# Layer one of a two-layer conditioned encoder: softmax sums from ScalarE's accumulator, spread as logarithms, in place of sums by matmul and a division

## The chip, the cores and the metric

The kernel runs on one core of one Trainium2 chip. The metric is the device time of one execution in microseconds (us). Engines are called as the profile calls them: PE (TensorE, matmuls), PEld (its weight loads), DVE (VectorE), ACT (ScalarE), POOL (GpSimd), SP (the queue of most transfers).

## The reference

Two layers on x of 32 batches x 128 tokens x 512 features, with a condition vector of 512 per batch. Cut to what matters (B = 32, N = 128, D = 512, 16 heads of 32):

```python
# layer one
h   = gamma(cond) * layernorm(x) + beta(cond)
q, k, v = split(h @ Wqkv.T + bqkv)             # 16 heads of 32 features
energy  = einsum('bhqd,bhkd->bhqk', q, k)
att     = softmax(energy, axis=-1) / D ** 0.5
h1      = einsum('bhqk,bhkd->bhqd', att, v) @ Wp.T + bp + x
x1      = (gamma(cond) * layernorm(h1) + beta(cond)) + h1
# layer two
h   = film(rmsnorm(x1), cond)                  # one attention head of 512 features
x2  = x1 + softmax(Q K^T * D**-0.5) V @ proj + b
out = x2 + gelu(film(rmsnorm(x2), cond) @ W1 + b1) @ W2 + b2
```

All is float32. Products that need the precision are made of three matmuls in the kernel: each operand is split into a high part (type fp32r) and a low part (the rest), and high x high, high x low and low x high are summed (`mm3`).

## The kernel before

The batches form eight groups of G = 4; a tile of a group has 128 partitions and 4 x 128 = 512 columns. Layer one is a loop of STEPS = 32: step s stands for group s // 4 and feature chunk c = s % 4, that is, four heads of 32 features for four batches at once. The order of the instructions on PE, DVE, ACT and POOL is the order in which the Python code writes them (`tc.manual_schedule`); only SP's queue is ordered by the framework. Each engine takes its own in order, and semaphores hold one back until its inputs and its buffers are ready.

For the softmax, a step works as a pipeline over three neighbouring steps:

- `qk0(s + 2)` makes queries and keys, features on partitions (12 matmuls each, copied out by ACT with the bias, L558).
- `energies(s + 1)` multiplies them per head and batch, with queries on partitions: 16 small matmuls into four PSUM banks `pse` (one for each head r; L575). DVE takes the negated maximum over the keys of each (L587) into `nm`, 128 x 16, and splits it into a high and a low part in `nmx` (L588, L589).
- `maxima(s + 1)` transposes `nmx` on PE (`psm`, L594); `spread_maxima(s + 1)` lays it out on DVE so that a matmul can add it to each column (L600).
- `scores0(s)` computes the scores once more with keys on partitions (`pst`, L616), into four banks that a matmul has first filled with the negated maxima (L612). `exponentials(s)` takes exp of each bank on ACT (L626): `e`.
- `heads_out(s - 1)` multiplies values by `e` (`pso`, L639). Four more matmuls multiply a constant `rootd`, 32 columns of sqrt(D), by `e` (`pss`, L644): the sum over the keys times sqrt(D), repeated on each head's 32 partitions. ACT takes the reciprocal as exp(-ln(.)) (L649, L650).
- `divided0(s - 1)`, on DVE, makes one Newton step for the reciprocal and multiplies (L657, L658, L659). ACT makes the high part for the projection (L661), POOL the low part (L662).

Beside this, each step carries one batch of the other work:

- The next input tile (`Turned`): `stats` and `norm` (DVE, with a power on POOL, L338), `halves` (ACT, L423, then a transposing transfer on SP), one step later `merge` (DVE, L432) and `rest` (four ACT activations, L449), then `high` (ACT, L461) and, at the next step's start, `low` (DVE, L465).
- The values of one batch (`values0`: 12 matmuls, copied by ACT, L542).
- From step 4, the projection of a batch of the group before (`End`: 12 matmuls `psp`, `add` on DVE, L693) and, one step later, the second normalization: `first` (statistics, a product on DVE, L707, an add on POOL, L708), `second` (DVE, L712), `third` (DVE, L721).
- From step 4 to 27, layer two's weights (`Weights`: ACT copies L936, POOL differences L943 and sums L929).

PSUM has eight banks in three pools: `mm_tile` (2), `s_tile` (2), `e_bank` (4). The scores take the two of `mm_tile` and the two of `s_tile`; the energies all four of `e_bank`. Between them the banks hold queries, keys, values, the heads, the sums, the maxima and the projection.

The order in the loop before, other work left out:

```python
energies(s + 1); scores0(s); heads_out(s - 1); exponentials(s)
divided0(s - 1)
run(q); maxima(s + 1); spread_maxima(s + 1); run(k)
run(end.stream())
run(values0(s - 1 + G))
```

Layer two's softmax (`softmax1`, L847) takes exp on 128 columns at a time with the negated maximum as bias and the accumulator's sum as second output.

Of the kernel before, what the change touches and what calls it, by code (L numbers as in the profile page):

```python
# [9 lines left out]
FP = mybir.dt.float32  # L10
# [28 lines left out]
RIGHT_LOW_LAST = ((0, 0), (1, 0), (0, 1))  # L39


@with_exitstack
def cond_seq_kernel(ctx: ExitStack, tc, x, condT, wcond, w0, w1, wk1, wm1, wm2, cols, rows, out):
# [68 lines left out]
    rootd = const.tile([P, HD], FP, name="rootd")  # L112
    nc.vector.memset(rootd, float(D) ** 0.5)
# [39 lines left out]
    def mm3(make, terms, done=None, by_part=False):  # L153

        if by_part:
            calls = [(a[pa], b[pb]) for pa, pb in RIGHT_LOW_LAST for a, b in terms]
        else:
            calls = [(a[pa], b[pb]) for a, b in terms for pa, pb in PARTS]
# [233 lines left out]
    class Turned:  # L392
# [66 lines left out]
        def high(self):  # L459
            if self.layer < 2:  # L460
                nc.scalar.copy(self.hi, self.dst)  # L461
# [42 lines left out]
    qk, vs, es, os_, mT = {}, {}, {}, {}, {}  # L504
# [45 lines left out]
    def qk0(s, by_part=False):  # L550
# [5 lines left out]
        for a, (nm, bias) in enumerate((("q", C_BQ0), ("k", C_BK0))):  # L556
            def done(ps, a=a, bias=bias):
# [5 lines left out]
                lambda nm=nm: (e_bank if nm == "q" and s > 1 else mm_tile)(f"ps{nm}{s}"),  # L563
# [5 lines left out]
    def energies(s):  # L569
# [14 lines left out]
        t = nmx  # L584
        nm = sm.tile([P, 4, G], FP, tag="nm", name=f"nm{s}")
        for r in range(4):
            nc.vector.tensor_reduce(nm[:, r], chunks(banks[r]), AX.X, ALU.max, negate=True)  # L587
        nc.vector.tensor_copy(t[:, :, :G].bitcast(FR), nm)  # L588
# [33 lines left out]
    def exponentials(s):  # L622

        for r in range(4):
# [4 lines left out]
    def heads_out(s):  # L629
# [5 lines left out]
        pso, pss = e_bank(f"pso{s}"), e_bank(f"pss{s}")  # L635
# [7 lines left out]
        for r in range(4):  # L643
            nc.tensor.matmul(  # L644
                pss[32 * r : 32 * r + 32], rootd, e[r], start=True, stop=True
            )

        w = p_tile(f"rs{s}")
        nc.scalar.activation(w, pss, AF.Ln)  # L649
        nc.scalar.activation(w, w, AF.Exp, scale=-1.0)  # L650
        es[s] = pso, pss, w

    def divided0(s):

        g, c = divmod(s, KC)
        pso, pss, w = es.pop(s)
        nc.vector.tensor_tensor(pss, pss, w, ALU.mult)  # L657
        nc.vector.tensor_tensor(w, pso, w, ALU.mult)  # L658
        nc.vector.scalar_tensor_tensor(w, pss, 2.0, w, ALU.subtract, ALU.mult, reverse0=True)  # L659
        hi, lo = (t[:, c] for t in os_[g])  # L660
        nc.scalar.copy(hi, w)  # L661
        nc.gpsimd.tensor_tensor(lo, w, hi.bitcast(FP), ALU.subtract)  # L662

    class End:
# [15 lines left out]
        def stream(self):  # L680
            g, i = divmod(self.b, G)

            def done(ps):
# [3 lines left out]
                lambda: mm_tile(f"psp{self.b}"),  # L687
                [(sub(os_[g], k, ts(i, P)), sub(W0["p"], k)) for k in range(KC)],
                done,
# [145 lines left out]
    def softmax1(g):  # L835
# [3 lines left out]
        nm = sm.tile([P, G], FP, tag="nm", name=f"nm1_{g}")  # L839
# [371 lines left out]
    with tc.manual_schedule(engines=ordered):  # L1211
# [65 lines left out]
        for k in range(KC):  # L1277
            product_end(k)
        for p in first:
# [361 lines left out]
```

## Time and profile before

| | |
|---|---|
| median of 3 runs | 1433.27 us (1433.21 to 1435.66) |
| the profiled execution | 1433.07 us, span 1431.3 us |
| busy, whole span | PE 1424.1, PEld 1144.8, DVE 1023.8, ACT 755.8, POOL 437.0 us |
| granted PE clock | 1.000 |
| layer one's loop | about 48 to 532 us of the span |
| sums matmuls, L644 | 256 rows of 592 ns, first at 63.5, last at 532.0 us |
| ACT exponentials, L626 | 128, mean 595 ns |
| DVE maxima, L587 | 128, mean 683 ns |

How to read the profile: an instruction's row has its start, its duration, its engine, its line of the kernel, and what it writes and reads by the program's names. Rows of neighbours on one engine overlap, so the time that an instruction costs its engine is better read from the start of one to the start of the next. Matmuls with 32 rows or 32 columns run side by side, four at a time. In a line of groups, "xN | busy, mean ns" is followed by the engine's idle time just before those instructions and by what ended it. In the chain that ended last each stretch is put down to the engine whose work or whose wait released the next.

### The profile page before, as it was taken

To read this page: it belongs to the slowest core of one execution; us is meant where nothing else is said; L and a number is where in the kernel's file an instruction comes from. 1 tells how busy PE (TensorE), PEld (TensorE's weight loads), DVE (VectorE), ACT (ScalarE), POOL (GpSimd) and SP (SyncE) were. 2 spreads that over 40 slices of the span, in tenths; PEclk is the share of its full clock that TensorE was granted. 3 is DMA by queue.
4 is the path that set the end of the run, shared out by engine and by line. 5 is a ranking of instruction groups with operands and counts; after the bars stand their busy time and mean duration, and the time that the engine had idled before them with its cause. 6 is when DMAs were issued, how large, how long until landed. Compare 5 with 4: busy or idle time off the path is not lost.

```text
span 1431.3 us, 24842 instructions
## 1 busy us (share of the span) xinstructions
PE 1424.1 (99%) x9224; PEld 1144.8 (80%) x9224; DVE 1023.8 (72%) x1909; ACT 755.8 (53%) x1392; POOL 437.0 (31%) x393
## 2 busy tenths in 40 slices
PE   9999999999999999999999999999999999999998
PEld 5777777777777768888888888888888888888887
DVE  6778889878888877999987766755566556743442
ACT  4566665665665546777874544434453444423231
POOL 0124555645645434566551223000030003110000
PEclk9999999999999999999999999999999999999999
DMA  8356788786667576778878867667693777735450
GB/s 313 106 185 160 194 209 221 190 199 176 165 170 189 136 236 184 179 214 232 206 203 338 285 198 255 231 191 220 192 333 122 226 217 223 275 125 179 151 184 30
DMA packets 227874, 287.83 MB, mean 201 GB/s; under 512 B 107396, under 2 KB 138244, under 8 KB 226216
## 3 DMA queue, kind: packets, MB, share of 16 engines
q1 hardware_dynamic: 209888, 211.68, 50.4%
q10 hardware_dynamic: 17864, 74.55, 16.1%
q8 instruction: 73, 1.20, 0.3%
q14 instruction: 49, 0.40, 0.1%
HBM read 193.18 MB, written 73.60 MB: 186 GB/s over the span
## 4 chain that ended last, share of the span: by engine, by line
PE 95%; DVE 3%; ACT 1%; POOL 0%; issue 0%; ACTq 0%; POOLq 0%; DVEq 0%
PE acc L1067 24%; PE psh L165 21%; PE psV L165 6%; PE psT L165 6%; PE psq L165 6%; PE psp L165 6%; PE psk L165 5%; PE psv L165 5%; PE pso L639 2%; PE pse L575 2%; PE pst L616 2%; PE pss L644 2%; PE pss L828 2%; PE pso L165 2%; PE psvp L767 1%; PE psm L744 1%
## 5 line engine op out<-in xcount | busy, mean ns | idle before, releaser
L338 POOL TENSOR_TENSOR rn<-vn,neghalf 128x1 f32<-128x1 f32 x96 | 71.1, 741 | 424.6 <-DVE vn L336 350.1
L423 ACT COPY tn<-x 128x1024 uint16<-128x1024 uint16 x90 | 93.9, 1044 | 68.6 <-DVE x L409 54.4
L1005 ACT ACTIVATE c<-c,col 128x512 f32<-128x512 f32 x64 | 46.4, 725 | 141.9 <-DVE c L1030 88.4
L587 DVE TENSOR_REDUCE nm<-pse 128x4 f32<-128x512 f32 x128 | 79.5, 683 | 45.2 <-PE pse L575 45.2
L1083 POOL TENSOR_TENSOR xe<-xe,row 128x512 f32<-128x512 f32 x32 | 45.3, 1445 | 200.8 <-DMA xe<-xs 144.5
L432 DVE COPY tn<-tn 128x1024 uint16<-128x1024 uint16 x90 | 92.2, 1024 | 0.9 <-DMA tn<-tn 0.9
L1020 DVE TENSOR_TENSOR c<-psh,ca 128x512 f32<-128x512 f32 x32 | 22.1, 691 | 87.0 <-PE psh L165 85.8
L626 ACT ACTIVATE e<-pst 128x512 f32<-128x512 f32 x128 | 65.3, 595 | 1.3 <-PE pst L616 1.3
L409 DVE TENSOR_SCALAR x<-x,rn 128x512 f32<-128x512 f32 x64 | 60.3, 943 | 7.8 <-POOL rn L338 7.2
L943 POOL TENSOR_TENSOR wml<-wm,wmh 128x512 fp32r<-128x512 f32 x28 | 35.5, 1276 | 99.3 <-ACT wmh L936 89.6
L326 DVE BATCH_NORM_STATS2 stn<-x 128x6 f32<-128x512 f32 x96 | 65.4, 682 | 0.1
L649 ACT ACTIVATE rs<-pss 128x512 f32<-128x512 f32 x32 | 19.1, 598 | 80.0 <-PE pss L644 80.0
L338 POOL TENSOR_TENSOR re<-ve,neghalf 128x1 f32<-128x1 f32 x32 | 31.7, 991 | 95.9 <-DVE ve L331 90.3
L449 ACT ACTIVATE tn<-tn,mods 128x128 f32<-128x128 f32 x128 | 52.6, 483 | 11.7 <-DVE tn L432 11.7
L1033 DVE TENSOR_TENSOR ca<-psh,ca 128x512 f32<-128x512 f32 x32 | 22.1, 691 | 42.4 <-PE psh L165 42.4
L449 ACT ACTIVATE tn<-tn,mod 128x128 f32<-128x128 f32 x104 | 42.9, 483 | 15.9 <-DVE tn L432 15.8
L678 POOL TENSOR_TENSOR xe<-xe,row 128x512 f32<-128x512 f32 x32 | 44.5, 1390 | 3.3 <-DMA xe<-in_x 2.8
L1005 ACT ACTIVATE cb<-cb,col 128x512 f32<-128x512 f32 x32 | 23.2, 725 | 41.6 <-DVE cb L1034 41.6
L1087 DVE TENSOR_TENSOR xe<-acc,xe 128x512 f32<-128x512 f32 x32 | 21.1, 688 | 32.4 <-PE acc L1067 32.4
L575 PEld LDWEIGHTS pse<-qk 32*128 32x128 f32 x1024 | 32.0, 186 | 12.2 <-issue 9.6
L1017 ACT COPY ca<-psh 128x512 f32<-128x512 f32 x32 | 18.4, 574 | 42.8 <-PE psh L165 42.2
L1026 DVE TENSOR_TENSOR cb<-psh,ca 128x512 f32<-128x512 f32 x32 | 22.1, 690 | 24.8 <-PE psh L165 24.6
(1387 smaller groups left out, 4703.7 us busy)
## 6 DMA issues: line engine op xcount, KB each, us to landing
mod<-mod SPq DMA_DIRECT2D x32, 512.0 KB, 5.2
ur<-ud SPq DMA_DIRECT2D x64, 256.0 KB, 4.2
xs<-xe SPq DMA_DIRECT2D x60, 256.0 KB, 2.9
xe<-xs SPq DMA_DIRECT2D x60, 256.0 KB, 3.1
x<-xs SPq DMA_DIRECT2D x59, 256.0 KB, 3.7
scw<-scw SPq DMA_DIRECT2D x32, 256.0 KB, 4.1
hTd<-tn SPq DMA_DIRECT2D x32, 256.0 KB, 6.7
hT<-hTd SPq DMA_DIRECT2D x32, 256.0 KB, 4.9
```

The source lines that it names most:

```text
L165: nc.tensor.matmul(st["ps"], *calls[j], start=(j == 0), stop=(j == n - 1))
L326: nc.vector.bn_stats(st, t)
L338: nc.gpsimd.tensor_tensor(r, v, neghalf, ALU.pow)
L409: nc.vector.tensor_scalar(X, X, r, None, ALU.mult)
L423: nc.scalar.copy(halves.rearrange("p (e d) -> p e d", e=2), X.bitcast(U16).rearrange("p (d e) -> p e d", e=2),)
L432: nc.vector.tensor_copy(self.a.bitcast(U16).rearrange("p (f e) -> p e f", e=2), self.t.bitcast(U16).rearrange("p (e f) -> p e f", e=2),)
L449: nc.scalar.activation(dst[:, c], self.a[:, ts(c, P)], AF.Identity, bias=m[:, q + B : q + B + 1], scale=m[:, q : q + 1],)
L575: nc.tensor.matmul(banks[r][:, ts(i, P)], q[32 * r : 32 * r + 32, ts(i, P)], k[32 * r : 32 * r + 32, ts(i, P)], start=True, stop=True,)
L587: nc.vector.tensor_reduce(nm[:, r], chunks(banks[r]), AX.X, ALU.max, negate=True)
L626: nc.scalar.activation(e, es[s][r], AF.Exp)
L1005: nc.scalar.activation(t[nm], t[nm], AF.Gelu, bias=col[:, C_B1 + f : C_B1 + f + 1], scale=1.0)
L1067: nc.tensor.matmul(accs[i], u[pa][:, ts(i, P)], wb[f // 4][pb][:, f % 4, :], start=(first and j == 0), stop=(last and j == len(PARTS) - 1),)
```

## The change

After the change, layer one's sums over the keys come from the energies, which have the queries on partitions. `totals(s, r)` takes exp in place, in the PSUM bank, 128 columns at a time: 16 ACT instructions in a step, each with the negated maximum as bias and with the accumulator's sum as output. `logs(s)` takes the logarithm of sqrt(D) times these sums, corrects it once (exp of its negative on ACT, two small operations on DVE) and subtracts it from the negated maxima. What is transposed and spread is then maximum and logarithm together, so that `exponentials` gives the finished attention. `heads_out` has no sums matmuls, `divided0` is gone; `heads_high` (ACT) and `heads_low` (DVE, before POOL) split the product straight from PSUM. The turned tile's high copy (`turned.high`) goes from ACT to DVE. Banks are dealt out anew: heads and queries in `mm_tile`, keys and values in `s_tile`, maxima and projection in `e_bank`. The order in the loop changes too.

The diff, without the part before the loop and the steps' rarer work:

```diff
-    rootd = const.tile([P, HD], FP, name="rootd")
-    nc.vector.memset(rootd, float(D) ** 0.5)
...
         if by_part:
-            calls = [(a[pa], b[pb]) for pa, pb in RIGHT_LOW_LAST for a, b in terms]
+            order = PARTS if by_part == "left" else RIGHT_LOW_LAST
+            calls = [(a[pa], b[pb]) for pa, pb in order for a, b in terms]
...
-                lambda nm=nm: (e_bank if nm == "q" and s > 1 else mm_tile)(f"ps{nm}{s}"),
+                lambda nm=nm: (s_tile if nm == "k" and s > 1 else mm_tile)(f"ps{nm}{s}"),
...
+    def totals(s, r):
+
+        banks, nm, total = sums0[s]
+        for i in range(G):
+            e = banks[r][:, ts(i, P)]
+            nc.scalar.activation(
+                e, e, AF.Exp, bias=nm[:, r, i : i + 1], scale=1.0,
+                accum_out=total[:, r, i : i + 1],
+            )
+
+    def logs(s):
+
+        _, nm, total = sums0.pop(s)
...
+        nc.scalar.activation(lg, total, AF.Ln, scale=ROOTD)
+        nc.scalar.activation(inv, lg, AF.Exp, scale=-1.0)
+        nc.vector.scalar_tensor_tensor(inv, total, ROOTD, inv, ALU.mult, ALU.mult)
+        nc.vector.scalar_tensor_tensor(lg, inv, -1.0, lg, ALU.add, ALU.add)
+        nc.vector.tensor_tensor(nm, nm, lg, ALU.subtract)
+        t = nmx
         nc.vector.tensor_copy(t[:, :, :G].bitcast(FR), nm)
         nc.vector.tensor_tensor(t[:, :, G : 2 * G], nm, t[:, :, :G], ALU.subtract)
...
-        pso, pss = e_bank(f"pso{s}"), e_bank(f"pss{s}")
+        pso = mm_tile(f"pso{s}")
...
-        for r in range(4):
-            nc.tensor.matmul(
-                pss[32 * r : 32 * r + 32], rootd, e[r], start=True, stop=True
-            )
-
-        w = p_tile(f"rs{s}")
-        nc.scalar.activation(w, pss, AF.Ln)
-        nc.scalar.activation(w, w, AF.Exp, scale=-1.0)
...
-        nc.vector.tensor_tensor(pss, pss, w, ALU.mult)
-        nc.vector.tensor_tensor(w, pso, w, ALU.mult)
-        nc.vector.scalar_tensor_tensor(w, pss, 2.0, w, ALU.subtract, ALU.mult, reverse0=True)
+        nc.scalar.copy(os_[g][0][:, c], es[s])
+
+    def heads_low(s):
...
-        nc.scalar.copy(hi, w)
-        nc.gpsimd.tensor_tensor(lo, w, hi.bitcast(FP), ALU.subtract)
+        nc.vector.tensor_tensor(lo, es.pop(s), hi.bitcast(FP), ALU.subtract)
...
-                lambda: mm_tile(f"psp{self.b}"),
+                lambda: e_bank(f"psp{self.b}"),
                 [(sub(os_[g], k, ts(i, P)), sub(W0["p"], k)) for k in range(KC)],
-                done,
+                done, "left" if i == 0 else False,
```

The loop's order after, as code (the steps' rarer work left out):

```python
scores0(s)
turned.high(nc.vector.tensor_copy); turned.low(nc.vector)
energies(s + 1)
exponentials(s, (0, 1)); totals(s + 1, 0); exponentials(s, (2, 3))
for r in range(1, 4): totals(s + 1, r)
heads_out(s - 1)
past.first(); past.sums(); new.stats(); end.bias(); end.more(); past.second()
ready.merge(); logs(s + 1); heads_high(s - 1)
run(q); run(k)
new.norm(); new.halves()
run(values)                      # steps 0 to 3: 7 of the 12, the rest behind the maxima
maxima(s + 1); spread_maxima(s + 1)
heads_low(s - 1); ready.rest(); past.third()
run(end.stream()); end.add()
weights.heads(wj); weights.tails(wj); weights.sums(wj + 1)
```

Before the loop, the energies, the sixteen exponentials and the logarithms of step 0 are put among the first values, queries and keys in the same way. The four products of layer two's value weights (`vp`, L767) are spread over steps 29 to 31 in another order, with their loads.

## The prediction

> **What bounds the kernel now.** I read the page first: the busy line, then the shares of the chain that ended last.
>
> ```profile
> PE 1424.1 (99%) x9224; PEld 1144.8 (80%) x9224; DVE 1023.8 (72%) x1909; ACT 755.8 (53%) x1392; POOL 437.0 (31%) x393
> ...
> PE 95%; DVE 3%; ACT 1%; POOL 0%; issue 0%; ACTq 0%; POOLq 0%; DVEq 0%
> ```
>
> The chain is PE's own stream almost everywhere, so a matmul that goes is worth its time, if nothing else becomes late. The change lies in layer one's 32 steps, so I asked for busy times over 19 whole steps in its middle (columns: stretch, length, PE, PEld, DVE, ACT, POOL).
>
> ```profile
> 151.62:443.42 291.80, 291.80 (x2984) 230.37 (x2984) 249.29 (x460) 177.73 (x325) 157.44 (x129) 1.00 0.73 192
> ```
>
> Divided by 19, a step is 15.36 us: PE busy for all of it, DVE 13.12, ACT 9.35, POOL 8.29, at full clock. DVE, not ACT, is next. Then the timeline of PE at a step's start:
>
> ```profile
> 243.76 1.17 PE L575 MATMUL pse<-qk 32*128 32x128 f32 x32
> 244.67 0.57 PE L612 MATMUL pst<-mT,over 32*128 32x512 f32 x4
> 244.99 1.15 PE L616 MATMUL pst<-qk 32*128 32x128 f32 x32
> 246.06 1.08 PE L639 MATMUL pso<-e,v 128*32 128x128 f32 x32
> 246.96 1.04 PE L644 MATMUL pss<-e,rootd 128*32 128x512 f32 x8
> 247.93 0.50 PE L165 MATMUL psq<-n_12h,w0qh 128*128 128x512 f32 x1
> ```
>
> From start to start: energies 0.91, scores 1.39, heads 0.90, sums 0.97.
>
> **PE: what goes.** The four sums matmuls (L644) leave each step: 246.96 to 247.93, 0.97. PE's step becomes 14.39. The other matmuls change place and bank, not number. If PE stayed the only bound, 32 x 0.97 = 31 us would go.
>
> **ACT: what comes.** The nearest row for an accumulating exponential on 128 columns is layer two's softmax:
>
> ```profile
> 570.48 0.37 ACT L847 ACTIVATE e<-pss,nm 128x128 f32<-128x128 f32 x1 [3.50 <-DVE nm L843]
> 570.74 0.19 ACT L847 ACTIVATION_READ_ACCUMULATOR e<-pss,nm 128x1 f32 x1
> 570.84 0.36 ACT L847 ACTIVATE e<-pss,nm 128x128 f32<-128x128 f32 x1
> ...
> 571.86 0.70 ACT L793 ACTIVATE T<-psT,cq 128x512 f32<-128x512 f32 x1
> ```
>
> Four pairs take 571.86 - 570.48 = 1.38, 0.345 a pair, though the durations add to 0.57. The 16 new pairs cost 5.52 a step. Theirs write to PSUM, which no ACT row here does; bounds are 0.26 (start to read, 570.74 - 570.48) and 0.57 (no overlap). I take 0.345: same form, and DVE's in-place product in PSUM (L657, 0.693) costs what the one into SBUF does (L658, 0.692).
>
> The logarithm and its exponential are now 128x16. From L649 (512 columns, 0.60) and L847 (128, 0.37) a line gives 0.3 each, 0.6 together (bounds 0.2 and 0.74). Three ACT spans leave:
>
> ```profile
> 232.65 0.60 ACT L649 ACTIVATE rs<-pss 128x512 f32<-128x512 f32 x1 [2.50 <-PE pss L644]
> 233.28 0.63 ACT L650 ACTIVATE rs<-rs 128x512 f32<-128x512 f32 x1
> 233.81 2.04 ACT L626 ACTIVATE e<-pst 128x512 f32<-128x512 f32 x4
> ...
> 244.59 0.62 ACT L461 CAST n_16h<-tn 128x512 fp32r<-128x512 f32 x1
> 245.11 0.62 ACT L936 CAST wmh<-wm 128x512 fp32r<-128x512 f32 x1
> ```
>
> L649 by 0.63, L650 by 0.53 (start to start), and L461, which moves to DVE, by 0.52. ACT: 9.35 - 1.68 + 5.52 + 0.6 = 13.8 a step, 4.4 more, under PE's 14.39 but no longer idle.
>
> By the Trainium skill (ScalarE: Activation LUTs, What ACT_TABLE_LOAD costs) an activation with a [128,1] bias takes about 280 ns plus 0.833 ns per column, and neighbours overlap by 93 ns: a rule against cutting four wide exponentials into sixteen, since each piece pays the fixed part again. For 128 columns that is an estimated 0.294, without the accumulator's read, so 4.7 a step where the row gives 5.52; by it the chain below would end 0.8 earlier, and PE would be the bound.
>
> **DVE and POOL.** L657, L658, L659 leave: 2.06 (234.73 to 236.79 in that step). In come the low part of the heads from PSUM (0.62 paced), the high copy of the turned tile (L1101's cast of this shape: 0.42) and three small operations at 0.21 (L588 to L589, 247.47 to 247.68). DVE: 13.12 - 2.06 + 0.62 + 0.42 + 0.63 = 12.73. POOL loses L662's 1.3.
>
> **The new chain.** All three engines fit, so the order decides. Logarithms need the step's sixteen pairs; the maxima's transpose, now behind the values' matmuls, needs the logarithms; the next scores need the transpose. On DVE the turned tile's normalization is queued behind the logarithms, and ACT's halves, values' copy and turned activations wait for it. DVE's rows, by mean, because they stretch:
>
> ```profile
> L432 DVE COPY tn<-tn 128x1024 uint16<-128x1024 uint16 x19 | 22.7, 1195 | 0.0
> L411 DVE TENSOR_SCALAR x<-x,mvn,rn 128x512 f32<-128x512 f32 x18 | 21.4, 1187 | 2.2 <-POOL rn L338 2.2
> L712 DVE SCALAR_TENSOR_TENSOR xe<-te,re,xe 128x512 f32<-128x512 f32 x19 | 20.1, 1057 | 0.0
> ```
>
> Time 0 is the start of the first pair. ACT: four pairs to 1.38, two exponentials (0.51 each) to 2.40, twelve pairs to 6.54, logarithm and exponential to 7.2. DVE: first maximum began at -0.75, four at 0.62 end at 1.75; first() 1.70, to 3.45; stats 1.0, to 4.45; second() waits for POOL (power 1.02, add 1.29, after 2.75) until 5.1, 1.06, to 6.16; merge 1.20, to 7.36; five dependent small ones to 8.4; normalization 1.19, to 9.6. ACT: halves 0.96, values' copy 0.47, four activations 1.65, to 12.75 with handoffs. DVE: high 0.42, low 0.62, next maximum 0.68, handoffs: the next first pair starts at 14.65. The other way round, through PE: transpose at 8.5, projection 2.72, scores 1.39, energies 0.91, maximum 0.68, handoffs: 14.5. So three limits lie at 14.39, 14.5 and 14.65; I take 14.65, a gain of 0.70.
>
> A rule against the moved copy: in the Trainium skill (SBUF — State Buffer, Who interferes with whom) DVE's two-port copies and GpSimd lock each other out for a whole instruction. The row that bears on it is L411, 530 ns at best and 1526 at worst in this trace. So the high copy lies between 0.42 and 1.42; I take 0.42, since at 12.75 POOL has done its adds and its next work waits for ACT's L936, which comes after. At the far end the step is 15.65.
>
> **Sum.** Against the profiled execution's own 1433.07 us (span 1431.3), 0.2 under the median of 1433.27.
> - Steps 6 to 27: 22 x 0.70 = -15.4.
> - Steps 0 to 3 (11.62, 13.64, 13.88, 14.67 now) have no projection, so PE gives ACT less cover: ACT's 6.97, 9.54, 9.02, 9.30 with the new work and 0.4 to 0.6 of waits make 13.2, 14.3, 13.9, 14.2: +1.6, +0.7, 0, -0.5. Steps 4 and 5 (17.22, 16.60) are long on PE: -0.9 each. Together 0.
> - The last four: three lose 0.97; step 30 (14.56) meets the chain: -0.1. Together -3.0.
> - Each fourth step, the projection needs the low heads, now last on DVE: 0.3 x 6 = +1.8.
> - Before the loop sixteen more pairs under PE's work: +0.5 (0 to 3).
>
> Total -16.1: 1417.
>
> **Rivals.**
> 1. PE alone stays the bound: the 0.26 of slack in my chain is not used, because DVE's stretches shrink with POOL's 1.3 gone. 22 x 0.97 + 3.0 and the steps 4, 5 on PE, with steps 0 to 3 at no loss: about -28, 1405; to 1402 with all 32. For it: PE is at 100% now. Against: 14.5 and 14.65 leave it no slack. Chance 0.15.
> 2. The saved matmuls are given back to DVE: second(), merge and normalization at their long forms (1.77, 1.64, 1.53) together add 1.5 to the chain; half of that makes 15.4 of a step, and the time 1433. Against: they seldom meet now. Chance 0.14.
> 3. Slower: the pairs don't keep 0.345 when they write to the bank they read. Each 0.044 more, sixteen times, eats 0.70, so 0.389 a pair decides. At 0.45 the chain is 16.3: 22 x 1.0 + 6 x 1.6 on the early steps, less 3.0: about +28, 1461; at 0.40, near 1437. For it: no row writes to PSUM from ACT. Against: the four paced pairs. Chance 0.20.
>
> **Numbers.** The forecast, 1417, has 0.51 with 1408 to 1427 of its own (the chain between 14.4 and 15.1). About 0.2% (2.9 us) is what a measurement can tell from none. Faster: forecast, rival 1 and nearly half of rival 2, 0.72; within 0.2%, 0.06; slower, rival 3 and a bit of 2, 0.22. The range takes in rivals 1 and 2 and the near end of 3: 1402 to 1443.
>
> **What would show it.** Right: no pss of L644, steps of 14.4 to 15.0 between energies, pairs at 0.345, ACT near 95% of a step, PE with gaps of 0.1 to 0.4 before the heads' matmuls or the scores. Wrong: pairs at 0.4 or more (rival 3); ACT idle before the halves for over 1.5 (rival 2); no PE gap at all (rival 1); steps 0 to 3 longer by over 5 in sum.

## The result, and the profile after

The changed kernel takes 1495.96 us (median of 4 runs, 1495.48 to 1499.81) against 1433.49 us for the kernel before on the same chip: ratio 1.0438, 95% interval 1.0418 to 1.0458. It is 62.5 us slower; 16 us faster was forecast. The profiled execution took 1495.56 us, its span is 1493.8 us at a granted clock of 0.992.

The page's busy line and the shares of the chain that ended last:

```profile
PE 1417.7 (95%) x8968; PEld 1139.3 (76%) x8968; DVE 1022.6 (68%) x1970; ACT 928.0 (62%) x2386; POOL 391.3 (26%) x361
PE 66%; ACT 19%; DVE 11%; issue 3%; DMA 2%; POOL 0%; SPq 0%; ACTq 0%; DVEq 0%; POOLq 0%
```

256 rows of PE matmuls went as planned (9224 to 8968), but PE now stands idle for 5% of the span, some 76 us, and the chain runs through ACT for 19% of it (before: 1%). The page's costliest groups show ACT's new work (columns: line, engine, operation, out<-in, count | busy us, mean ns of one | idle before, releaser):

```profile
L596 ACT ACTIVATE pse<-pse,nm 128x128 f32<-128x128 f32 x512 | 174.7, 341 | 46.6 <-DVE nm L588 34.2
L596 ACT ACTIVATION_READ_ACCUMULATOR pse<-pse,nm 128x1 f32 x512 | 100.0, 195 | 0.0
```

Means say nothing of pace. The timeline of ACT does (start, duration):

```profile
297.71 0.34 ACT L596 ACTIVATE pse<-pse,nm 128x128 f32<-128x128 f32 x1 [1.05 <-DVE nm L588]
297.97 0.19 ACT L596 ACTIVATION_READ_ACCUMULATOR pse<-pse,nm 128x1 f32 x1
298.20 0.34 ACT L596 ACTIVATE pse<-pse,nm 128x128 f32<-128x128 f32 x1
...
301.98 0.34 ACT L596 ACTIVATE pse<-pse,nm 128x128 f32<-128x128 f32 x1
302.24 0.19 ACT L596 ACTIVATION_READ_ACCUMULATOR pse<-pse,nm 128x1 f32 x1
302.33 0.33 ACT L596 ACTIVATE pse<-pse,nm 128x128 f32<-128x128 f32 x1
```

Within a bank the next pair starts 298.20 - 297.71 = 0.49 after the last, and only behind the accumulator's read; from the fourth pair of one bank to the first of the next it is 302.33 - 301.98 = 0.35. In the trace the second to fourth pair of each bank carry a wait on ACT's own semaphore, the one that the accumulator's read raises, and they start just behind the end of the neighbour's read (297.97 + 0.19 = 298.16, then 298.20). Layer two's pairs, on which the forecast's 0.345 rests, carry none. The trace does not say which instruction such a wait is for; that it is the neighbour's read is inferred from the start.

What PE waited for in the kernel after (total, times, longest), and three of its DVE groups over 18 steps in the middle; then the second of them in the kernel before:

```profile
PE psm L619 <- DVE nmx L614: 43.6, 25, 2.9
PE psvp L784 <- ACT lg L607: 8.3, 1, 8.3
```

```profile
L432 DVE COPY tn<-tn 128x1024 uint16<-128x1024 uint16 x18 | 33.2, 1842 | 0.0
L465 DVE TENSOR_TENSOR n_20l<-tn,n_20h 128x512 fp32r<-128x512 f32 x4 | 6.8, 1689 | 0.1
L411 DVE TENSOR_SCALAR x<-x,mvn,rn 128x512 f32<-128x512 f32 x18 | 9.7, 541 | 0.0
```

```profile
L465 DVE TENSOR_TENSOR n_20l<-tn,n_20h 128x512 fp32r<-128x512 f32 x4 | 2.7, 684 | 0.0
```

The late engine ahead of PE is most often DVE with the maxima (nmx): 43.6 of the 76 us, 1.74 to 1.77 in nearly every middle step. On DVE the merge went from a mean of 1.20 (the prediction shows its line) to 1.84, and the turned tile's low part from 0.68 to 1.69, with the same shapes. Other operations went the other way: the normalization (L411) from 1.19 to 0.54, `second()` from 1.06 to 0.75.

Where the time lies, by the starts of the energies (step n runs from energies n+1 to energies n+2, as in the prediction; us):

| | to energies(0) | steps -1 to 5 | steps 6 to 27 (median step) | from there to layer two |
|---|---|---|---|---|
| before | 33.7 | 102.5 | 337.9 (15.35) | 91.1 |
| after | 34.2 | 128.7 | 364.9 (16.53) | 100.4 |
| difference | +0.5 | +26.2 | +27.0 | +9.2 |

From the start of layer two on, both kernels take the same (866.0 and 865.6). The change puts each step's scores ahead of the next energies, so 1.4 of the +26.2 is counted there and missing at the end.

A part of the difference is PE's clock. In the kernel before, PE has no wait over 0.5 us between the first energies and layer two, and the granted clock there is 1.00. In the kernel after it is 0.50 in four stretches: 65.77 to 72.60, 120.38 to 123.80 and 154.52 to 157.93 (all in the early steps) and 567.53 to 577.77 (step 30). The first begins within a PE wait of 2.9 us, the second and third 1.3 and 0.3 us behind waits of 1.3 and 3.6, the last within the wait of 8.3. One stretch (columns as in the prediction, then clock, DMA share, GB/s), two matmuls in it, and two of the same form in the next step:

```profile
154.52:157.93 3.41, 3.41 (x9) 2.64 (x9) 0.00 (x0) 1.20 (x2) 0.00 (x0) 0.50 1.15 272
154.65 0.63 PE L165 MATMUL psv<-w0vl,n_8h 128*128 128x512 f32 x1
155.07 0.63 PE L165 MATMUL psv<-w0vh,n_8l 128*128 128x512 f32 x1
...
170.82 0.39 PE L165 MATMUL psv<-w0vh,n_8h 128*128 128x512 f32 x1
171.05 0.39 PE L165 MATMUL psv<-w0vl,n_8h 128*128 128x512 f32 x1
```

From start to start 0.42 against 0.23. PE is busy for 18.7 us of the four stretches; at full clock that work would take half, so an estimated 9 of the 62.5 us come on top of the waits themselves, 6.6 of them in the early steps. Not every wait is followed by such a stretch: the 1.75 of the middle steps are not. No run tries what decides it.

### The profile page after: what moved, and what is told of

It is laid out like the page before. It is cut to its first block, busy times and chain, and to the rows that moved or that the text cites. A ratio compares the mean times of both kernels' runs of the same rounds, so it can differ in the third digit from the quotient of the medians.

```text
span 1493.8 us, 25238 instructions
## 1 busy us (share of the span) xinstructions
PE 1417.7 (95%) x8968; PEld 1139.3 (76%) x8968; DVE 1022.6 (68%) x1970; ACT 928.0 (62%) x2386; POOL 391.3 (26%) x361
## 3 DMA queue, kind: packets, MB, share of 16 engines
q10 hardware_dynamic: 17864, 74.55, 15.1%
## 4 chain that ended last, share of the span: by engine, by line
PE 66%; ACT 19%; DVE 11%; issue 3%; DMA 2%; POOL 0%; SPq 0%; ACTq 0%; DVEq 0%; POOLq 0%
PE acc L1084 23%; PE psh L165 20%; ACT pse L596 15%; PE psV L165 5%; PE psT L165 5%; PE psp L165 3%; ACT e L651 2%; PE pss L845 2%; PE pso L165 1%; DVE nm L588 1%; DVE xe L710 1%; PE psvp L784 1%; DVE scw L738 1%; PE psv L165 1%; DMA wc<-in_wcond 1%
## 5 line engine op out<-in xcount | busy, mean ns | idle before, releaser
L596 ACT ACTIVATE pse<-pse,nm 128x128 f32<-128x128 f32 x512 | 174.7, 341 | 46.6 <-DVE nm L588 34.2
L338 POOL TENSOR_TENSOR rn<-vn,neghalf 128x1 f32<-128x1 f32 x96 | 62.9, 655 | 466.3 <-DVE vn L336 348.1
L432 DVE COPY tn<-tn 128x1024 uint16<-128x1024 uint16 x90 | 101.9, 1132 | 3.7 <-DMA tn<-tn 3.7
L596 ACT ACTIVATION_READ_ACCUMULATOR pse<-pse,nm 128x1 f32 x512 | 100.0, 195 | 0.0
L651 ACT ACTIVATE e<-pst 128x512 f32<-128x512 f32 x128 | 69.0, 594 | 18.2 <-PE pst L641 17.7
L619 PE MATMUL psm<-ident,nmx 128*128 128x128 f32 x32 | 10.4, 324 | 49.2 <-DVE nmx L614 43.6
L619 PEld LDWEIGHTS psm<-ident,nmx 128*128 128x128 f32 x32 | 4.5, 140 | 62.1 <-DVE nmx L614 54.6
L609 DVE SCALAR_TENSOR_TENSOR einv<-tot,einv 128x16 f32<-128x16 f32 x32 | 5.6, 175 | 62.2 <-ACT einv L608 62.2
L1034 ACT COPY ca<-psh 128x512 f32<-128x512 f32 x32 | 18.4, 574 | 41.5 <-PE psh L165 40.9
```

What stands on the lines that cost most here:

```text
L338: nc.gpsimd.tensor_tensor(r, v, neghalf, ALU.pow)
L432: nc.vector.tensor_copy(self.a.bitcast(U16).rearrange("p (f e) -> p e f", e=2), self.t.bitcast(U16).rearrange("p (e f) -> p e f", e=2),)
L596: nc.scalar.activation(e, e, AF.Exp, bias=nm[:, r, i : i + 1], scale=1.0, accum_out=total[:, r, i : i + 1],)
L651: nc.scalar.activation(e, es[s][r], AF.Exp)
```

## The experiments

Times are medians; ratios stand against the kernel before, run beside them, with 95% intervals. "Early" is steps -1 to 5, "step" the median of steps 6 to 27. Line numbers shift by one or two between the kernels. Each edit is against the kernel after, except the one that is said to be against the kernel before; the runs under "The second limit" and "What was left" all have the first run's edit in them. Steps are read from one profiled execution of each kernel.

### The pairs' pace

**Pairs written into SBUF instead of in place.**

```diff
+        mT[s] = sm.tile([P, G, P], FR, tag="mT", name=f"mT{s}", bufs=1)
...
-                e, e, AF.Exp, bias=nm[:, r, i : i + 1], scale=1.0,
+                mT[s][:, i], e, AF.Exp, bias=nm[:, r, i : i + 1], scale=1.0,
```

> Edit: the sixteen accumulating exponentials of a step write their values to the SBUF tile that later takes the spread maxima, and no longer into the PSUM bank that they read. Theory A (each pair after the first of a bank waits for the one before it, since both touch one PSUM tile: 0.49 us from start to start in place of 0.345, twelve times a step, 1.74): pairs at 0.345 to 0.36, steps 6 to 27 at 14.7 to 15.0 in place of 16.52, whole time 1442 to 1452 in place of 1496. Rival B (the new order of DVE and PE is what is late, ACT's pairs only fill the wait): steps stay over 16, time above 1485.

Measured 1449.42, ratio 1.0115 (1.0099 to 1.0131): 46.5 us of the 62.5 come back. Early 115.0, step 15.18. ACT's timeline:

```profile
305.88 0.37 ACT L597 ACTIVATE mT<-pse,nm 128x128 fp32r<-128x128 f32 x1 [1.03 <-DVE nm L588]
306.15 0.19 ACT L597 ACTIVATION_READ_ACCUMULATOR mT<-pse,nm 128x1 f32 x1
306.24 0.36 ACT L597 ACTIVATE mT<-pse,nm 128x128 fp32r<-128x128 f32 x1
```

0.36 a pair, 0.34 later in the row; the next one starts while the accumulator is still being read. Here too twelve of the sixteen pairs carry a wait on ACT's own semaphore, so such a wait alone costs nothing; whom it is for seems to matter. An estimated 5 of the 46.5 us are PE's clock: the stretches at 0.50 shrink from 18.7 us of PE's work to 7.9.

**In place, but twelve of the pairs go round three banks,** so that no pair follows one in its own bank. Were PSUM as the destination slow, these would stay slow.

```diff
-    def totals(s, r):
+    def totals(s, *rs):
...
         for i in range(G):
...
+            for r in rs:
+                e = banks[r][:, ts(i, P)]
...
-                for r in range(1, 4):
-                    totals(s + 1, r)
+                totals(s + 1, 1, 2, 3)
```

> Edit: still in place in PSUM, but the twelve pairs of the last three banks go around the banks (bank 1, 2, 3, 1, ...), so that two neighbours never touch one bank; the four of bank 0 stay in a row. Theory A (a wait for the neighbour in the same bank): nine of twelve waits go, about 0.13 each, steps 6 to 27 near 15.3, time about 1460. Rival C (ACT itself is slower when it writes into PSUM, whatever the neighbour): pairs stay at 0.49, step 16.5, time 1496.

Measured 1454.09, ratio 1.0144 (1.0128 to 1.0161), step 15.27. In one step, the first bank's pairs (not turned) and then the turned ones:

```profile
307.76 0.34 ACT L597 ACTIVATE pse<-pse,nm 128x128 f32<-128x128 f32 x1 [1.01 <-DVE nm L588]
308.25 0.34 ACT L597 ACTIVATE pse<-pse,nm 128x128 f32<-128x128 f32 x1
...
310.55 0.35 ACT L597 ACTIVATE pse<-pse,nm 128x128 f32<-128x128 f32 x1
310.89 0.36 ACT L597 ACTIVATE pse<-pse,nm 128x128 f32<-128x128 f32 x1
```

The same instruction into the same memory: 0.49 behind a neighbour in its bank, 0.34 otherwise. So it is the neighbour in the same tile, not PSUM as the place that is written. Reading one bank in a row costs nothing either (the pairs into SBUF do that). Whether the program's wait or the bank itself holds back a pair that reads and writes there, no run separates; the start just behind the accumulator's read speaks for the wait.

**One wide exponential a bank in place of four pairs;** this kernel leaves out three quarters of the sums (a bank's four run into one), and its exponentials don't wait for the maxima.

```diff
-        for i in range(G):
-            e = banks[r][:, ts(i, P)]
-            nc.scalar.activation(
-                e, e, AF.Exp, bias=nm[:, r, i : i + 1], scale=1.0,
-                accum_out=total[:, r, i : i + 1],
-            )
+        nc.scalar.activation(
+            banks[r], banks[r], AF.Exp, bias=neghalf, scale=1e-3,
+            accum_out=total[:, r, 0:1],
+        )
```

> Leaves out three quarters of the sums: each bank is taken by one exponential over all 512 columns with a constant bias (four ACT instructions a step in place of sixteen pairs), everything else in the new order. It shows the floor of the new order without ACT's new work. Theory A: ACT falls to about 10 of a step, steps 6 to 27 at PE's 14.4, time 1496 minus 22 x 2.1 minus 8 to 20 on the early steps: 1425 to 1442 (the wait for the load in step 30 stays in it). Rival B (the new order itself): steps above 15.5, time above 1465.

Measured 1438.87, ratio 1.0039 (1.0024 to 1.0054). ACT works 10.57 a step instead of the 13.37 of the pairs in SBUF (steps 6 to 27), and the step stays at 15.19, their 15.18. So there is a second limit, close under the first, and it isn't ACT. Early falls by 10.0 against that run, to 105.0: there ACT's work is on the path. (3.6 of the 10.0 are step 5, where the wait for the feature copies is gone too.)

### What the removed matmuls are worth, and the late load

**The kernel before, without the sums' matmuls** (the edit is against the kernel before); the division takes the heads in place of the sums, and a copy stands for the logarithm.

```diff
-        for r in range(4):
-            nc.tensor.matmul(
-                pss[32 * r : 32 * r + 32], rootd, e[r], start=True, stop=True
-            )
...
-        nc.scalar.activation(w, pss, AF.Ln)
+        nc.scalar.activation(w, pso, AF.Copy)
...
-        nc.vector.tensor_tensor(pss, pss, w, ALU.mult)
+        nc.vector.tensor_tensor(pss, pso, w, ALU.mult)
```

> Leaves out the sums: the kernel before in its own order, without the four sums matmuls; ACT copies the heads in place of the sums' logarithm, the rest of its work as before. It prices the saving alone. If the 0.97 are on the path in all steps: steps at 14.4, time 1434 minus 29 to 31, 1403 to 1405. If a second limit lies close under 15.35 (DVE at 13.1 of a step and its waits): steps at 14.6 to 15.2, time 1410 to 1428.

Measured 1415.95, ratio 0.9882 (0.9844 to 0.9921): 18.5 us by the medians (11 to 22 by the interval), not the 31 of 32 x 0.97. The usual step is 14.48, 0.87 less than before, but six of the 22 take 14.8 to 16.0 and one takes 18.39. In that one PE waits 0.95 and 0.43 and then has a granted clock of 0.50 for 3.41 us; what holds the others was not looked into.

**Chunk 1 of layer two's value weights loaded a step earlier,** ahead of two loads of 1 MB.

```diff
-            if s == STEPS - 2:
-                vp_load(1)
...
             if s == STEPS - 3:
+                vp_load(1)
                 vp_load(2)
```

> Edit: only the load of the second chunk of layer two's value weights moves, from step 30 to the end of step 29, ahead of the two 1 MB loads that now stand before it in SP's queue. If the 8.3 us that PE stands idle in step 30 are this load's wait: PE's gap before those products falls below 2 us and the time drops by 7 to 8, to 1488. If step 30 is bound by ACT's chain anyway: under 3 us, 1493 to 1496.

Measured 1488.3, ratio 1.0388 (1.0364 to 1.0413), 7.7 less than after; the stretch behind step 27 goes from 100.4 to 93.3. The profile's releaser for that wait (ACT lg L607, 8.3) was not its cause: PE waited for the chunk. Its load was issued at 561.36 behind two of 1 MB in SP's queue and landed at 572.16, and PE went on at 572.30; with the load earlier PE's longest wait there is 2.0.

### The second limit

Both groups of DVE that had stretched run beside GpSimd: the merge beside `end.bias()` (L696), the low part beside the weights' low part (L961). These runs move one or the other.

**The turned tile's high and low parts behind the maxima,** in three steps of four.

```diff
-            if turned:
+            if turned and (s + 2) % KC == 0:
                 turned.high(nc.vector.tensor_copy)
...
                 energies(s + 1)
+            if turned:
+                turned.high(nc.vector.tensor_copy)
+                turned.low(nc.vector)
+                turned = None
```

> Edit: e1_sbuf, and on DVE the turned tile's high and low parts come behind the four maxima in the steps whose queries don't need them (18 of the steps 6 to 27's kind, not each fourth). With ACT relieved, e1_sbuf and e5_wide both stop at 15.18 a step, so what ends last there is not ACT. Theory D (the low part, blocked behind POOL's weight subtraction for 1.70 in place of 0.62, delays the first maximum, and ACT stands idle for 1.05): the idle time goes, those steps fall to 14.4 to 14.7, each fourth stays at 15.2, time 1449 minus 10 to 14: 1435 to 1439. Rival E (the limit of 15.18 lies elsewhere, in merge or the normalization): under 3 us.

Measured 1455.25, ratio 1.0143 (1.0122 to 1.0164), step 15.71. The low part falls to 0.69, but the merge, still 1.84, now ends 1.5 later than ACT's exponential of the logarithm (with the pairs in SBUF alone it is 0.5): the step is longer, not shorter.

**The weights' work (`sums`, `heads`, `tails`) behind `new.halves()`.**

```diff
+            if 0 <= wn < KC:
+                weights.sums(wj)
+                weights.heads(wj)
+                weights.tails(wj)
             values = values0(s - 1 + G) if s <= B - G else []
...
-                weights.heads(wj)
-                weights.tails(wj)
-                weights.sums(wj + 1)
```

> Edit: e1_sbuf, with the weights' work (POOL's sum, ACT's high copy, POOL's subtraction) moved from the step's end to behind the halves, the low part left ahead of the maxima. Theory D (the low part is late because POOL's subtraction locks it out): the low part falls from 1.70 to about 0.69 and all steps 6 to 27 to 14.4 to 14.8, time 1449 minus 8 to 16: 1433 to 1441. Rival F (the low part takes 1.70 for another reason, the high copy before it or its wait for ACT): steps stay at 15.2, time 1446 to 1451.

Measured 1456.94, ratio 1.0157 (1.013 to 1.0185), step 15.75; 14.65 to 15.4 in steps that have no such work. GpSimd and DVE in one step, side by side:

```profile
297.45 1.47 POOL L696 TENSOR_TENSOR xe<-xe,row 128x512 f32<-128x512 f32 x1
298.87 1.78 POOL L947 TENSOR_TENSOR wm<-wm 128x512 f32<-128x512 f32 x1
```

```profile
297.68 1.86 DVE L432 COPY tn<-tn 128x1024 uint16<-128x1024 uint16 x1
299.42 1.26 DVE L610 SCALAR_TENSOR_TENSOR einv<-tot,einv 128x16 f32<-128x16 f32 x1
```

The merge ends 0.62 after L696 does (298.92 to 299.54), nearly its own length when nothing is beside it (0.74, below). Then L610, 16 columns wide and 0.16 elsewhere, ends when L947 does (300.68, 300.65). So one engine holds the other up (the lock, below), and it goes on to the next operation.

**The merge behind the normalization.**

```diff
-            if ready and not last:
-                ready.merge()
             if not last:
                 logs(s + 1)
...
                 new.halves()
+            if ready and not last:
+                ready.merge()
```

> Edit: e1_sbuf, and the merge of the transposed tile comes behind the normalization on DVE, no longer ahead of the logarithms' small operations. In e1_sbuf, e6_low and e7_weights the merge takes 1.84 to 1.86, locked behind POOL's add of the projection's bias, and the logarithms start when it ends: 0.4 us after ACT's exponential in e1_sbuf, 1.4 in e6_low. Theory G (the merge ahead of the logarithms is the second wait): the small operations start with ACT's exponential, steps 6 to 27 fall by 0.4 to 0.6 from 15.18, time 1449 minus 8 to 13: 1436 to 1441. Rival H (the merge is only moved, and ACT's four activations or the maxima's spread wait for it instead): within 3 us of 1449.

Measured 1453.61, ratio 1.0130 (1.011 to 1.015): step 14.87, 0.31 better than with the merge ahead, but early 119.6 (+4.6), and two middle steps stand out: 16.26, and 20.45 (step 12), in which PE waits 3.9 and then has a clock of 0.50 for 3.41 us. Steps 6 to 27 together take 336.2, against 336.3 with the pairs in SBUF alone.

**All moves at once,** two ways: load, low part, weights and feature copies; then load, merge, low part, feature copies and `first[1].rest()` earlier.

> The change with all repairs: exponentials into SBUF (e1), the load (e3), the low part behind the maxima (e6), the weights' work moved (e7), and layer two's features' transposes of step 5 behind the values. If each removes its own wait: 1449 minus 8 (load), minus 12 to 16 (steps), minus 3 (step 5): 1422 to 1428, under the kernel before. If the repairs of e6 and e7 work on one wait and another limit stands at 15.0: 1432 to 1438.

> All together: exponentials into SBUF (e1), load (e3), merge behind the normalization (e10), low part behind the maxima in the steps that allow it (e6), the features' transposes of step 5 behind the values, and the second input tile's turn ahead of the third values before the loop. Theory G with D (with the merge out of the way, the earlier maxima count): steps at 14.4 to 14.7 but each fourth near 14.8; 1449 minus 8 (load), 3 (step 5), 1 (before the loop), 22 x 0.5 to 0.7: 1421 to 1427, under the kernel before. If a third limit stands at 15: 1433 to 1438.

The first measured 1467.86, ratio 1.0233 (1.0208 to 1.0257), steps of 14.7 to 18.4: merge and L610 both locked (1.85, 1.23) one after the other. The second measured 1449.52, ratio 1.0108 (1.0091 to 1.0125), step 15.11, with one of 20.49. With the merge gone from the place beside L696, L610 takes 0.95 there:

```profile
362.46 0.95 DVE L610 SCALAR_TENSOR_TENSOR einv<-tot,einv 128x16 f32<-128x16 f32 x1 [0.24 <-ACT einv L609]
```

Moving DVE's operations only hands on the lock. So the next runs moved GpSimd's.

**`end.bias()` ahead of `past.first()`,** with the pairs in SBUF, the earlier load and `cond_features()` behind the halves; then the same with the weights' work moved.

```diff
+            if end:
+                end.bias()
             if past:
                 past.first()
...
             if end:
-                end.bias()
                 end.more()
```

> Pairs into SBUF, w1c chunk 1 loaded a step earlier, cond_features() behind the halves, and GpSimd's end.bias() issued ahead of past.first(), so that its add (L696, 1.46) runs while VectorE reduces maxima from PSUM and not while it merges. All of the work is done. Theory F (the second limit is VectorE locked out by GpSimd in the merge ahead of the logarithms): L432 falls from 1.85 to 0.75 with nothing else stretched, the steps from 15.18 to 14.5 (14.3 to 14.8), step 5 from 20.51 to 16.2: 1449.4 - 7.7 - 4.4 - 22 x 0.6 = 1424 (1418 to 1432), faster than the kernel before. Theory G (the lock is handed on to whichever two-input operation VectorE runs beside GpSimd, as in the runs that moved the low parts and the weights' work): the steps stay at 15.0 to 15.2 and the time is 1434 to 1438, no better than before. If the add waits for xe's load (6.4 from issue to landing) it delays the power behind it: steps over 15.2.

> As the run with end.bias() ahead of past.first(), and the weights' work of a step (sums, heads, tails) behind the halves besides, as in the run that moved it alone. All of the work is done. Theory F: the turned tile's low part L465 falls from 1.70 to 0.69 as well; ScalarE then sets the step or TensorE does, 14.4 to 14.6: 1420 to 1425. Theory G: steps of 15.0 to 15.7 in which the small operations or the normalization take over the lock; 1436 to 1445.

Measured 1442.88, ratio 1.0066 (1.005 to 1.0083), and 1444.85, ratio 1.0074 (1.0061 to 1.0087). The step is 14.82 in the first, with DVE's rows

```profile
296.99 0.74 DVE L432 COPY tn<-tn 128x1024 uint16<-128x1024 uint16 x1
298.36 0.17 DVE L610 SCALAR_TENSOR_TENSOR einv<-tot,einv 128x16 f32<-128x16 f32 x1 [0.62 <-ACT einv L609]
```

The merge at 0.74, and DVE now waits for ACT's logarithm: the lock was the second limit, 15.18 to 14.82. But single steps of 16 to 19.5 (5, 8, 11, 14) eat the rest, and in each GpSimd's add stands waiting for its load (6.05, 3.52, 4.68, 3.95). In step 5:

```profile
141.05 1.29 POOL L696 TENSOR_TENSOR xe<-xe,row 128x512 f32<-128x512 f32 x1 [6.05 <-DMA xe<-in_x]
```

### What was left

**The four 1 MB copies on ACT's queue behind the load of xe; then also all four wide exponentials ahead of the pairs; then also the weights' work moved.**

```diff
             end = End(s - G, True, nc.scalar) if s >= G else None
+            q2, late = divmod(s - 1 - W_FIRST, 3)
+            if not late and 0 <= q2 < 4:
+                nc.scalar.dma_start(out=w2d[q2], in_=wm2[:, q2])
...
-            exponentials(s, (0, 1))
+            exponentials(s, range(4))
```

> As the run with end.bias() ahead of past.first(), but the four 1 MB copies w2d<-wm2, issued from ScalarE's queue at the ends of steps 4, 7, 10 and 13, stand behind the next step's load of xe instead of ahead of it. All of the work is done. Theory Q: in that run the steps 5, 8, 11 and 14 (19.46, 16.03, 17.21, 16.47 against 14.8) are long because GpSimd's add stood waiting for xe's load (3.5 to 6.1 us) behind such a copy, and the power, second() and the logarithms' small operations behind it: with the order turned they come to 14.8 to 15.0 (step 5: 16.2), 8 us less: about 1435 (1432 to 1438). If the copies cost through the shared DMA engines and not through the queue's order, the four steps stay long and the time 1443.

> As the run with the copies behind xe's load, and ScalarE does all four wide exponentials ahead of the sixteen pairs. All of the work is done. Theory S (with the pairs at 0.345 and the merge at 0.75 it is ScalarE's chain that sets the 14.81 us: it works 13.35 and stands 1.0 to 1.2 before the first pair for VectorE's first maximum): the two exponentials fill that wait, the steps fall to 14.4 to 14.55, where TensorE's own 14.39 bounds them: 1435 - 22 x 0.3 = 1428 (1425 to 1433), faster than the kernel before. If the steps stay at 14.8, something behind the pairs sets them (VectorE's maxima or TensorE's projection), and the time stays at 1435.

> As the run with the exponentials ahead of the pairs, and the weights' work behind the halves, so that the turned tile's low part runs at 0.69 and not at 1.70. All of the work is done. If VectorE is still part of the step's chain: another 0.1 to 0.2 a step less, 1425 to 1428. If TensorE is the bound by then, no difference within 2 us. Where the moved work locks another of VectorE's operations, 2 to 6 us more.

Measured 1441.71 (ratio 1.0053, 1.0036 to 1.0071), 1441.46 (1.0046, 1.0026 to 1.0065) and 1442.16 (1.0056, 1.0036 to 1.0076). In the first, steps 8 and 11 come down to 14.81 and 14.85 as expected, and step 5 to 17.3, but steps 12 and 14 now take 18.69 and 17.40: in step 12 xe's load landed 9.5 after its issue, with no such copy ahead of it, and the add waited 4.6. The queue's order was one cause of late loads, not the only one. The add stands ahead of the power, so every late load delays the logarithms; the next runs take it away from there. With the exponentials together the shortest steps are 14.47, what the kernel before takes without its sums' matmuls (14.48); long ones, up to 19.2, remain (the profiled execution, 1448, is the slowest of eight; the median is 1441). In the longest of these runs (18.69 in the first, 18.79 and 19.15 in the second) PE's clock is 0.50 for 3.41 us behind a wait of 2.4 to 2.9.

**The add held back instead:** GpSimd first copies one column of the normalized tile, and so starts the add only when DVE is through the logarithms; then with the weights' work behind it; then with the low part behind the maxima.

```diff
                 new.norm()
+                if end:
+                    gate = sm.tile([P, 1], FP, tag="gate", name=f"gate{s}")
+                    nc.gpsimd.tensor_copy(gate, new.X[:, 0:1])
                 new.halves()
+            if end:
+                end.bias()
```

> Pairs into SBUF, all four wide exponentials ahead of them, chunk 1 loaded a step earlier, cond_features() behind the halves; end.bias() on GpSimd behind a one-column copy of the normalized tile, which makes it wait until VectorE's logarithm operations and normalization are done (the add then runs beside VectorE's operations that read PSUM). All of the work is done. Theory F+Q (what remained in the runs with end.bias() first were GpSimd's waits for xe's load, up to 9.6 us after its issue): no step over 16 behind step 5, the steps 14.47 without and 15.1 with a locked low part (L465 beside L961): about 1432 (1427 to 1437), no worse than the kernel before. If long steps of 16 to 19 stay, it isn't that wait, and the time is 1440.

> As the run with the add held back, and the weights' work behind that add. All of the work is done. Theory F: the low part at 0.69, steps of 14.47 throughout: 1423 to 1428, faster than the kernel before. If the later sums and parts on GpSimd reach into the next merge or lock the low part instead, steps of 15 and 1432 to 1438.

> As the run with the add held back, and the turned tile's high and low parts behind the maxima in the steps that don't need them at once. All of the work is done. Theory F: the lock of the low part no longer stands ahead of the maxima, steps of 14.47 except each fourth (15.1): 1424 to 1429. If it pushes first(), the power and the merge into the logarithms, as the run that moved the low parts alone did, steps of 15 and over: 1435 to 1442.

Measured 1433.02 (11 runs), ratio 0.9991 (0.9983 to 1.0); 1442.99, 1.006 (1.0048 to 1.0072); 1432.43 (12 runs), 0.999 (0.9978 to 1.0002). GpSimd in the first of them:

```profile
303.40 0.18 POOL L1424 COPY gate<-x 128x1 f32<-128x1 f32 x1 [2.46 <-DVE x L411]
303.54 1.29 POOL L696 TENSOR_TENSOR xe<-xe,row 128x512 f32<-128x512 f32 x1
```

With the add behind the normalization, at a price of 0.18 of GpSimd's idle time, the steps of 17 to 19 behind step 5 are gone in this profile: most take 14.47 or 15.1, in turn, three take 16.0 to 16.4, and layer two starts at 563.9 against 565.3 before. The low part is still locked (1.65) in short and long steps alike, so that isn't what sets the longer ones; what does was not settled. No run has the add in its new place without the copy, so how much the place does and how much the copy is open. In the second run the lock goes to `past.third()` (L739, mean 1.35 and up to 1.79, against 0.74 in the first), and one step of 18.73 is left. The first and third are no slower than the kernel before, and faster by no more than a measurement can tell.

Over the parts of the span:

| | early | steps 6 to 27 | from there to layer two |
|---|---|---|---|
| before | 102.5 | 337.9 | 91.1 |
| after | 128.7 | 364.9 | 100.4 |
| pairs in SBUF | 115.0 | 336.3 | 96.1 |
| add first | 115.9 | 331.9 | 90.4 |
| add held back | 110.6 | 328.4 | 91.0 |

## Why the prediction was wrong

**The step that failed first is ACT's price of a pair.** 0.345 was read off layer two's pairs as "same form". They read PSUM and write slices of an SBUF tile; these read and write slices of one PSUM tile, and each starts only when the one before it is through. 12 of 16 pairs cost 0.49: 12 x 0.145 = 1.74 a step, and 14.65 + 1.74 = 16.39 against 16.53 measured. That is rival 3 in its size (its 0.45 a pair is nearly the mean here, (12 x 0.49 + 4 x 0.35) / 16 = 0.455, and its chain 16.3) but not in mechanism: writing to the bank that is read is not slower, as the pairs that go round the banks show (0.34). The row of DVE's in-place product, used as support, could not speak for ACT's waits.

**The second is DVE's work by means and best cases.** The low part was taken at 0.62 and is 1.69, the merge at 1.20 and is 1.84; this is rival 2's mechanism for one of the three operations that it named (`second()` and the normalization became shorter), and for one that it didn't. It hid behind the first error: in the kernel after, the merge ends 1.2 before ACT's exponential of the logarithm. Rival 2 was argued down by "they seldom meet now"; in the new order they meet in every step, since DVE reaches the merge as GpSimd starts its add. The moved high copy, for which the prediction did weigh the lock, kept its 0.42 in 18 of 20 steps; the rule was applied to the one operation that moved on paper, not to those whose neighbours moved. The Trainium skill (SBUF — State Buffer, Who interferes with whom) names all of them: copies in a two-port mode block with GpSimd for a whole instruction, and operations with two SBUF inputs contend with GpSimd's reads. The rows agree, and show the second kind held up to the end of GpSimd's instruction too, down to 16 columns (0.16 to 1.26).

**Where the chain's own working held, in part by luck.** With pairs at 0.345 and the merge unlocked the step is 14.82, forecast 14.65. But in that run the low part takes 1.69 (forecast 0.62), the merge 0.75 (1.20), the normalization 0.54 (1.19) and `second()` 0.75 (1.06): errors in both directions that nearly cancel. With ACT's wait for the first maximum filled, the short steps are 14.47, where the ledger put PE at 14.39; the median with the add held back is 14.75. The small logarithms were over-priced (0.22 each, not 0.3). The ledger's 0.97 was nearly right for a single step (0.87), and too much for their sum: even with nothing added, 18.5 us is what the matmuls are worth here. Rival 1's "about -28" is a slip as well: its terms, 22 x 0.97 + 3.0 and 0.97 for steps 4 and 5 each, make 26.3.

**The early steps were mis-sized most:** +0.5 before the loop and 0 over the first six steps were forecast, +26.2 came. Writing the pairs to SBUF takes 13.7 of it away (128.7 to 115.0), an estimated 5 of them through the clock (PE's work in stretches at 0.50 falls from 13.2 us to 3.4). Of the 12.5 that are left then, 1.4 are the counting, and some 4 are step 5's wait for the feature copies in ACT's queue (step 5 takes 20.51 with the pairs in SBUF, 15.92 and 16.14 in the two runs with all moves, these copies among them). The wide exponentials, shorter and without the wait for the maxima, take 10.0 off, step 5's 3.6 included: the chain through ACT is nearly all of it. Steps 0 to 3 with the pairs in SBUF take 13.24, 15.04, 14.53 and 15.32, against 13.2, 14.3, 13.9 and 14.2 forecast: ACT's busy time and a few tenths were too little there, since the logarithms, behind all pairs, now stand ahead of the transpose. The step before them, at 18.91 against 14.83 (1.4 of it the counting), was put at +0.5. 8.1 remain with the add held back; which of ACT's operations carries them was not tried.

**The last steps:** -3.0 was forecast, +9.2 came. 7.1 of it is one load's place in SP's queue (100.4 to 93.3). The prediction didn't follow the DMAs that the change moves.

Put together, rival 3's 1461 (28.6 us) lacked 26.2 - 9.6 = 16.6 in the early steps, 27.0 - 22 = 5.0 in the middle and 9.2 + 3.0 = 12.2 at the end: 33.8, which makes 1494.8 (measured in that execution: 1495.6). This is bookkeeping by parts of the span, not a proof of the causes. All three engines "fit" in 14.39; what came instead are waits, rows stretched by a neighbour, and PE at half its clock behind its waits, and a ledger of busy times taken from the kernel before sees none of them.

## What to carry to other kernels

A price is taken over from a row only with its operands' places and its waits: look at what the instruction waits for, its own engine included, and if slices of one tile are read and written in place, try another tile as destination or another order. When a step is reordered, lay GpSimd's timeline beside VectorE's for the new order and ask of every copy and every operation with two SBUF inputs, not only of the moved ones, what runs next to it; then move GpSimd's instruction, not VectorE's, and hold it back with a cheap dependency rather than put it first, where it waits for its load. Follow every DMA that a moved step issues to its place in the queue. And look at the granted clock behind each long wait of TensorE: the wait's own length may not be all that it costs.

## What the runs showed of the hardware that was not expected

- ACT pairs of 128 columns with accumulator: 0.34 apart into SBUF or into PSUM behind a neighbour in another bank, 0.49 in place behind a neighbour in the same bank.
- GpSimd holds up even a 128x16 operation of DVE for the rest of its own instruction: 0.16 became 0.95 and 1.26.
- GpSimd's one-column copy takes 0.18 us, cheap enough to serve as a gate.
- The 256 KB load of xe landed 2.5 to 13.7 us after its issue (13.7 in the run with the merge behind the normalization); what decides it was not tried.
- Behind or within some of TensorE's waits (0.95 to 8.3 us), and not behind others of 1.75, the granted clock was 0.50 for 3.41 us or a multiple of it; matmuls 0.23 apart were then 0.42 apart.
